# A four-layer metaformer on one core: the first and last chunk of each mixer rewritten, and the feed-forward stages put in another order

## The chip, the core and the metric

The kernel runs on one core of one Trainium2 chip. Its time is the device time in microseconds (us) of one execution; three runs of the kernel before gave 8925.73, 8928.08 and 8933.33 us, median 8928.08. The core has a TensorE (PE) with a separate record for its weight loads (PEld), a VectorE (DVE), a ScalarE (ACT), a GpSimd (POOL) and a SyncE (SP) that mostly issues DMAs. Each engine works its own instructions in the order of its queue and waits on semaphores for the others. "L578" is line 578 of the kernel before.

## What is computed

An input of 64 images, each of 11 x 11 = 121 positions with 128 values, goes through four layers, all in fp32:

```python
for l in range(4):
    x = x + mixer[l](layernorm(x))
    x = x + ffn[l](layernorm(x))
```

The mixer is the same in all four layers. It treats the 121 positions as channels and 256 inner features as the time axis of a recurrence with 16 states, for two sets k of parameters:

```python
xc, z = split(x @ in_proj_w.T)                 # 256 features each
t = silu(conv1d(xc, conv_w) + conv_b)          # three taps over the 121 positions, 256 -> 256
dt, B, C = split(einsum(t, x_proj_w[k]))
delta = softplus(dt @ dt_proj_w[k] + dt_proj_b[k])
h = scan(exp(delta * A[k]), delta * B * t)     # along the 256 features; 121 channels x 16 states
y[k] = (h * C).sum(states) + Ds[k] * t
yn = layernorm(y[0] + flip(y[1]))              # over the 121 channels
out = (yn * gelu(z)) @ out_proj_w.T
```

The feed-forward part differs. Layer 0 has 64 experts that choose their tokens: a gate of 128 x 64, a softmax over the 121 tokens of an image, the top 8 tokens of each expert pooled, an MLP 128-512-128 for each expert, and its output spread back over those tokens. Layers 1 and 2 have an RNN: `wx = BatchNorm(x @ W.T)`, then `y[t] = sigmoid(wx[t] + y[t-1] @ V.T)` over the 121 positions. Layer 3 is a spectral transform: the positions fall into four bands (0-15, 15-30, 30-60, 60-121), each with convolutions by 16 filters and their sign-alternated twins, channel matrices M for each filter, three autoregressive terms M_u, and weights for the bands that are made from a softmax.

## The kernel before

The mixer (class `Conv`) works through the 64 images in eight chunks of 8 images. For each chunk and each k, the 121 channels are taken two at a time (8 images x 16 states = 128 partitions for a channel), 61 pairs, which gives 2 x 8 x 61 = 976 steps to a layer. A step makes `delta` for its pair in PSUM with two bf16 products (`rows`, L557), `exp(delta * A)` with two ACT instructions (`exps`, L570), multiplies the drive by B on POOL (`times_b`, L546, one instruction for two steps), and runs one scan of 512 elements on DVE (`scan`, L578) into a buffer `H`. PE then multiplies by C and sums the states (`by_c`, L599), `keep_y` (L614 on DVE, L616 on ACT) gathers this in `yst`, and `store_y` (L631) writes it to a DRAM tensor `yD`. The drive comes back from DRAM copied 16 times (`load_u`, L534, tile `ub`); `load_r` (L507) and `load_bc` (L516) fetch delta, B and C.

What feeds a chunk is made in three groups of closures. `lead(c)` loads the images (`begin`, L190), takes mean and variance on DVE (L196, L201), makes the reciprocal root by `rsqrt` (Ln at L175, Exp at L176), normalises on ACT, transposes on PE, copies on ACT, and then runs the convolution: for each image four products into a PSUM tile `pc` (three taps and one with the bias row, L232), for each two images a copy to `t` (`convd`, L235), and silu for all (`silu`, L239). `steps(c, k, start, apart, late)` makes delta for four pairs of images: `project` (PE, L267), `parts` (relu and abs, L274), `e` (exp, L277, and +1, L279), `ln` (L283), `less` and `delta` (DVE, L286 to L290), `first` (bf16 part of delta, L295), `u` (POOL, L299), `rest`, `second`, `third` (the two further bf16 parts, L302 to L308), `store` (two DMAs, L311 and L312, to `dD` and `uD`). Each closure has a step number, and `apart` says how many steps lie between one pair of images and the next. The PSUM tile `pd` has one buffer and is held from `project` to `delta`. `aside(c)` makes B and C (product L333, copy L338, store L341 to `bcD`) and the Ds term (L351 to L361, stored to `sD`). What follows a chunk is `gate` (gelu(z)) and `tail(c)`: load of the Ds term (`ts`, L411) and of y (L413), transposes to a PSUM tile `pk`, sum and layer norm of y (L426 to L448), product with the gate (L453), load of x (`xo`, L462), output projection (L472), addition (L475) and store to a DRAM tensor `mid` (L485), in four blocks, one for each half of the features and each half of the images.

Inside the mixer the program order is the order written by hand (`manual_schedule`). In the loop, the closures of the next chunk and of the chunk before are laid between the 976 steps by `lay` and `lay_at`. Only two places are not beside the loop: the first chunk of a layer, ahead of step 0,

```python
self.do([begin] + norms + convs)
self.do([f for _, f in self.steps(0, 0, 0, 8, 1)] + aside[: 3 * CB // 2])
```

and the last chunk's `tail`, behind step 976. `apart` is 8 in this call, `late` is 1. A layer begins with the mixer's constants (`weights`, L95 to L148: twelve loads and the products made of them) and its buffers (L155 to L166, with memsets of `da`, `yst` and others).

The feed-forward functions run without a written order; a scheduler orders their instructions by priority, which falls in program order. X, all 64 images, is loaded in eight DMAs at L1159 (each of 8 images, directly behind the mixer), and stored in eight at L1162. `layer_norm` (L46 to L58) normalises 8 images in eight instructions, the last at L58. `moe_layer` runs the gate for groups of 8 images (L784 to L814) on 64 partitions, then the experts (L820 to L846), then the output (L851 to L858). `rnn_layer` runs a front over groups of 8 images (product with W at L886 to L890, batch statistics, `wx` copied by ACT), puts `wx` into PSUM with products of 512 columns (L914), and then runs the 121 steps: product with V (L920) and sigmoid (L923). `stu_layer` loads filters, M_u and a weight matrix W, and for each group of 8 images: layer norm and transposes, the products with the filters (`pu`, L1072) and with M (`acc`, L1075, L1077), and four products of W (L1092) with 2048 columns of M, written to a DRAM tensor `KD` (L1094); then three bands whose matrices are read back from `KD` (L1106), and the addition into X for all images (L1127 to L1129).

## Time and profile before

The profiled execution took 8938.7 us; its span is 8936.9 us, at a mean granted TensorE clock of 0.754. The table gives where its parts lie in us from the start of the span. The channel loop is counted from its first scan (L578) to its last.

| layer | ahead of the first scan | channel loop | last chunk, to the last store of mid | feed-forward part, to its last store |
|---|---|---|---|---|
| 0 | 0 - 108.4 | 108.4 - 1767.7 | - 1817.1 | - 2223.0 (experts) |
| 1 | 2223.0 - 2330.5 | - 3984.2 | - 4036.7 | - 4285.0 (RNN) |
| 2 | 4285.0 - 4392.8 | - 6052.0 | - 6101.5 | - 6348.7 (RNN) |
| 3 | 6348.7 - 6465.2 | - 8113.0 | - 8163.0 | - 8936.9 (spectral) |

Over the whole span the busy shares are:

```profile
PE 6165.8 (69%) x83464; PEld 3518.2 (39%) x83464; DVE 6233.4 (70%) x8294; ACT 5776.4 (65%) x12747; POOL 5849.9 (65%) x3155
```

A window's line in what follows gives its start and end, its length, then the busy time of each engine in it with the number of instructions in brackets, the granted PE clock as a share of the full one, the mean busy share of the 16 DMA engines, and GB/s. A timeline's line gives the start of an instruction, its duration, its engine and line, the operation, output and inputs, and in square brackets how long the engine had been idle before it and what ended that.

### The profile page before, as it was taken

The page shows a single profiled execution, that of the slowest core. Times are in us where ns is not written, and L with a number is a line of the kernel's source. Part 1 is how long each engine was busy: PE and PEld are TensorE (multiplying, and loading weights), DVE is VectorE, ACT ScalarE, POOL GpSimd, SP SyncE. Part 2 cuts the span into 40 slices and gives each one's busy share as a digit, 9 for nine tenths or more (in the row PEclk, how much of TensorE's full clock was granted, in tenths as well). Part 3 has the DMA queues.
Part 4 walks back from the last instruction along what each step waited for, and adds up shares of the span by engine and source line. Part 5 has one row for each costly group of instructions (what it writes and reads, how often), then busy time and mean ns, then how long its engine had stood idle before and what let it go on. Part 6 is the DMA issues. An engine that isn't in the chain of part 4 may idle for free. (4 is left out here: it accounts for less than half of the span.)

```text
span 8936.9 us, 208810 instructions
## 1 busy us (share of the span) xinstructions
PE 6165.8 (69%) x83464; PEld 3518.2 (39%) x83464; DVE 6233.4 (70%) x8294; ACT 5776.4 (65%) x12747; POOL 5849.9 (65%) x3155
## 2 busy tenths in 40 slices
PE   5667767637567777766577777765567777765998
PEld 2333434327233434333234444443334444433445
DVE  5888888753588888872478888883288888884220
ACT  5888888631688878862478887872288788873210
POOL 5888888700588888860488888880188888892000
PEclk7777777657677777775687777775577777777999
DMA  6889898815688899970489999991288999994111
GB/s 148 213 227 223 225 222 227 195 55 166 152 220 225 225 222 224 228 183 25 128 215 219 224 225 222 223 227 41 61 218 225 228 226 224 224 234 106 35 32 42
DMA packets 926426, 1604.62 MB, mean 180 GB/s; under 512 B 139455, under 2 KB 611587, under 8 KB 923587
## 3 DMA queue, kind: packets, MB, share of 16 engines
q1 hardware_dynamic: 924171, 1589.17, 71.1%
q8 instruction: 655, 10.73, 0.5%
q14 instruction: 320, 2.62, 0.1%
q10 hardware_dynamic: 1280, 2.10, 0.1%
HBM read 1300.49 MB, written 290.52 MB: 178 GB/s over the span
## 5 line engine op out<-in xcount | busy, mean ns | idle before, releaser
L546 POOL TENSOR_TENSOR ub<-ub,Bt 128x1024 f32<-128x1024 f32 (+1 forms) x1984 | 4563.0, 2317 | 770.6 <-DMA ub<-uD 544.5
L578 DVE TENSOR_TENSOR_SCAN H<-da,ub 128x512 f32<-128x512 f32 (+1 forms) x3904 | 4499.2, 1200 | 229.4 <-POOL ub L546 104.3
L570 ACT ACTIVATE da<-da,A 128x255 f32<-128x255 f32 x7744 | 3390.5, 446 | 1112.9 <-PE da L557 938.2
L557 PE MATMUL da<-R,pick 120*128 120x255 bf16 x7744 | 1793.5, 326 | 885.6 <-DVE H L578 708.3
L599 PE MATMUL yb<-H,Cz 128*16 128x64 f32 x65536 | 1734.5, 251 | 548.8 <-ACT yst L616 361.0
L599 PEld LDWEIGHTS yb<-H,Cz 128*16 128x16 f32 x65536 | 1173.6, 111 | 1597.1 <-issue 844.5
L557 PEld LDWEIGHTS <-pick 120*128 120x128 bf16 x7744 | 601.0, 104 | 1590.4 <-issue 818.1
L161 POOL MEMSET t<- 128x2048 f32 x4 | 7.2, 1805 | 914.4 <-DMA mid<-X 914.4
L232 PE MATMUL pc<-w_conv,xnT 128*121 128x256 f32 x1536 | 502.7, 431 | 65.7 <-ACT t L235 65.7
L614 DVE TENSOR_TENSOR yst<-yst,yb 128x512 f32<-128x512 f32 (+2 forms) x640 | 342.0, 552 | 274.5 <-PE yb L599 274.0
L299 POOL TENSOR_TENSOR u<-relu,t 128x512 f32<-128x512 f32 x256 | 327.3, 1279 | 294.8 <-DVE relu L290 294.8
L267 PE MATMUL pd<-t,w_dt 122*128 122x512 f32 x512 | 392.9, 861 | 130.1 <-ACT t L239 68.5
L616 ACT COPY yst<-yb 128x512 f32<-128x512 f32 (+2 forms) x640 | 330.5, 542 | 107.6 <-DMA yD<-yst 47.6
L286 DVE SCALAR_TENSOR_TENSOR pd<-w,pd 128x512 f32<-128x512 f32 x256 | 175.8, 687 | 301.7 <-ACT w L279 301.7
L308 POOL TENSOR_TENSOR d<-relu,d 128x512 bf16<-128x512 f32 x256 | 297.0, 1160 | 80.5 <-ACT d L305 80.2
L232 PEld LDWEIGHTS pc<-w_conv,xnT 128*121 128x121 f32 x1536 | 273.7, 210 | 130.8 <-ACT t L235 96.5
L453 POOL TENSOR_TENSOR y<-y,g 128x484 f32<-128x484 f32 x128 | 155.5, 1215 | 240.4 <-ACT y L448 240.4
L302 POOL TENSOR_TENSOR relu<-relu,d 128x512 f32<-128x512 f32 x256 | 297.3, 1161 | 7.8
L333 PE MATMUL pb<-t,x_bc 121*64 121x512 f32 x256 | 184.5, 811 | 133.7 <-ACT bc L338 102.7
L1055 DVE COPY U<-pu 128x488 f32<-128x488 f32 x128 | 85.3, 667 | 273.6 <-PE pu L1072 273.6
L523 POOL TENSOR_TENSOR Cz<-Cp,own 128x512 f32<-128x512 f32 x256 | 274.4, 1072 | 0.0
L1057 ACT COPY U<-pu 128x488 f32<-128x488 f32 x128 | 72.8, 569 | 296.5 <-PE pu L1072 296.5
(211 smaller groups left out, 7529.1 us busy)
## 6 DMA issues: line engine op xcount, KB each, us to landing
ub<-uD SPq DMA_DIRECT2D x1920, 512.0 KB
dD<-d SPq DMA_DIRECT2D x256, 384.0 KB
R<-dD SPq DMA_DIRECT2D x192, 420.0 KB
uD<-u SPq DMA_DIRECT2D x256, 256.0 KB
sD<-s SPq DMA_DIRECT2D x128, 256.0 KB
ts<-sD SPq DMA_DIRECT2D x64, 512.0 KB
yD<-yst SPq DMA_DIRECT2D x512, 60.5 KB
y<-yD SPq DMA_DIRECT2D x128, 242.0 KB
```

The costliest lines, as they stand in the source:

```text
L232: nc.tensor.matmul(pc, lhs, rhs, start=(j == 0), stop=(j == 3))
L267: nc.tensor.matmul(s["p"], self.w_dt[:, k, :], tb[: D + 1], start=True, stop=True)
L299: nc.gpsimd.tensor_mul(s["u"], s["relu"], tb)
L302: nc.gpsimd.tensor_sub(s["relu"], s["relu"], s["d"][:, 0, :])
L308: nc.gpsimd.tensor_sub(s["d"][:, 2, :], s["relu"], s["d"][:, 1, :])
L546: self.nc.gpsimd.tensor_mul(x, x, self.bc[m, "Bt"].unsqueeze(1).to_broadcast([128, n, L]))
L557: self.nc.tensor.matmul(self.da[g % RING][:, j, 1:], self.pick[:n, d % 5].rearrange("p n b -> p (n b)"), self.R[m, d // 35][:n, d % 35 // ...
L570: self.nc.scalar.activation(x, x, AF.Exp, scale=self.A[:, m % 2, d : d + 1])
L578: self.nc.vector.tensor_tensor_scan(self.H[dq % 2][:, :n, p - DQ[dq][0]], self.da[g % RING].rearrange("p j l -> p (j l)")[:, :n], x.rearra ...
L599: self.nc.tensor.matmul(self.yb[32 * q : 32 * q + 16, slot % 8, :, :, :w], self.Cz[slot // 8][:, place % 64 : place % 64 + 2, :].rearrange ...
L614: nc.vector.tensor_add(dst, dst, src)
L616: nc.scalar.copy(dst, src)
```

## The change

**Layer norm of the feed-forward parts.** `layer_norm` takes mean and variance with `bn_stats` and `bn_aggr`, one of each for an image, makes the reciprocal root with Ln and Exp, and normalises with one ACT instruction for an image.

**Constants.** `weights` is cut into the loads (`weights`) and what is made of them (`made`). The feed-forward functions get an argument `load`: called in them, it issues the loads of the next layer's mixer constants, and then the eight loads of X. `made()` runs inside the feed-forward part. `cw`, `cs` and `cv` are their pools.

**First chunk of a layer.** The two `H` buffers serve as scratch memory (`spare`), as the scan doesn't use them yet. The convolution has three taps and four PSUM buffers (`da`), the bias is added by DVE from a tile that a broadcast DMA fills, and silu is done for two images at a time. In `steps` the four pairs of images each have their own PSUM and SBUF tiles and stand 2 steps apart, with the closures of B and C among them. `da`'s first column is cleared after that, and `yst` no longer.

**Last chunk of a layer.** `last` takes the place of `tail(NC - 1)`: loads of `ts` and `xo` one step after the loop's end, `load(0)` (y of the first half of the features) at step 12 after it, transposes and the gate's half of the projection (`ahead`) before `load(1)`, and four blocks skewed against each other (`finish`).

**Experts.** The gate works on 128 partitions (four images for each half) and goes through the groups with norm, front, softmax and back each one group apart; two multiplications of a group go to POOL, one copy from ACT to DVE. The pool of expert weights has four buffers for three. The output part is loaded in quarters and goes by row halves.

**RNN.** The front is skewed by one group, and `wx` is copied by DVE. In layer 2, the new function `stu_matrices` makes the matrices of layer 3's spectral part: 64 products of W with 256 columns of M, one of them issued after each step of the recurrence, written to `cx.KD`.

**Spectral part.** The products with W and their loads are gone from it, `scale_weights` is taken out into a function, the layer norm and transposes of a group run one group ahead, the last group's products come after the bands, X of the other groups is added before them, and the K tiles have three buffers for two.

```diff
 def layer_norm(cx, pool, dst, src, eps):
-    nc.vector.reduce_sum(mean, src, axis=AX.X)
...
-    nc.vector.tensor_mul(dst, dst, bcast(rstd, C))
+    for i in range(G):
+        nc.vector.bn_stats(st[:, i, :], src[:, i, :])
+    for i in range(G):
+        nc.vector.bn_aggr(mv[:, i, :], st[:, i, :])
+    nc.scalar.activation(r[:, 0, :], mv[:, :, 1], AF.Ln, bias=eps[:D])
+    nc.scalar.activation(r[:, 0, :], r[:, 0, :], AF.Exp, scale=-0.5)
+    nc.vector.scalar_tensor_tensor(r[:, 1, :], mv[:, :, 0], -1.0, r[:, 0, :], ALU.mult, ALU.mult)
+    for i in range(G):
+        nc.scalar.activation(
+            dst[:, i, :], src[:, i, :], AF.Identity, bias=r[:, 1, i : i + 1], scale=r[:, 0, i : i + 1]
+        )
...
 # Conv.lead
+        taps = 3 if c == 0 else 4
...
+            if c == 0:
+                s["bias"] = self.spare[0][:D, :L]
+                nc.sync.dma_start(s["bias"], self.cx.a[f"L{self.l}_conv_conv_b"].to_broadcast([D, L]))
...
-                s["pc"] = self.ps_d.tile([D, 2, L], F32, name="pc", tag="pd")
+                s["pc"] = self.da[b // 2][:D] if c == 0 else self.ps_d.tile([D, 2, L], F32, name="pc", tag="pd")
...
         def convd(b):
-            nc.scalar.copy(self.t[:D, b : b + 2, :], s["pc"])
+            if c > 0:
+                nc.scalar.copy(self.t[:D, b : b + 2, :], s["pc"])
+                return
+            bias = s["bias"].unsqueeze(1).to_broadcast([D, 2, L])
+            nc.vector.tensor_add(self.t[:D, b : b + 2, :], s["pc"], bias)
...
 # Conv.steps
+        alone = c == 0 and k == 0
...
+                if alone:
+                    at = 1024 * b + 512 * ("relu", "abs", "w", "ln").index(n)
+                    return self.spare[1][:, at : at + 512]
...
+                if alone:
+                    s["p"] = self.da[b // 2].rearrange("p j l -> p (j l)")
+                else:
+                    s["p"] = self.ps_d.tile([128, 512], F32, name="pd", tag="pd")
...
 # Conv.last, new
+        def sides():
+            for q in range(2):
+                nc.sync.dma_start(ts[q], self.sD[c, :, 4 * q : 4 * q + 4, :])
...
+        def load(h):
+            for q in range(2):
+                nc.sync.dma_start(s[q, h]["y"], self.yD[c, 128 * h : 128 * h + 128, q * D4 : q * D4 + D4])
...
+        def finish():
...
+            for k in range(6):
+                if k < 4:
+                    b = s[blocks[k]]
+                    nc.vector.tensor_add(b["y"], b["y"], b["pk"][:, :D4])
...
+                    self.rsqrt(b["r"], b["mv"], self.cx.eps5)
+                if 0 < k < 5:
+                    q, h = blocks[k - 1]
...
+                    nc.gpsimd.tensor_mul(b["y"], b["y"], self.g[:, h, q * D4 : q * D4 + D4])
+            for q in range(2):
+                proj(q, True)
+                nc.sync.dma_start(self.dst(c * CB + 4 * q, 4), xo[q].rearrange("p (b c) -> p b c", c=C))
...
 # Conv.run
-        self.do([f for _, f in self.steps(0, 0, 0, 8, 1)] + aside[: 3 * CB // 2])
+        bc = [(3 * i // 3 + 1.5, f) for i, f in enumerate(aside[: 3 * CB // 2])]
+        self.do([f for _, f in sorted(self.steps(0, 0, 0, 2, 1) + bc, key=lambda x: x[0])])
+        for x in self.da:
+            self.nc.vector.memset(x[:, :, 0:1], 0.0)
...
+        sides, load, ahead, finish = self.last(NC - 1)
+        self.at(G + 1, sides)
+        self.at(G + 12, lambda: load(0))
...
-        self.do([f for _, f in sorted(self.tail(NC - 1), key=lambda x: x[0])])
+        ahead()
+        load(1)
+        finish()
...
 # moe_layer
+        xn, pr = {0: norm(0)}, {}
+        for g in range(NG + 2):
+            if g + 1 < NG:
+                xn[g + 1] = norm(g + 1)
+            if g < NG:
+                pr[g] = front(xn[g])
+            if 1 < g:
+                back(g - 2, xn[g - 2])
+            if 0 < g <= NG:
+                softmax(g - 1, pr[g - 1])
+            if g == 1:
+                made()
...
 # stu_matrices, new: 8 rounds of 2048 columns, called by next(beside, None) after each step of layer 2's recurrence
+            for j in range(0, CC, PC):
+                pa = ps.tile([R0[3], PC], F32, name="pa", tag="mm")
+                nc.tensor.matmul(pa, W, loaded[c0][:, j : j + PC], start=True, stop=True)
+                nc.vector.tensor_copy(ka[:, j : j + PC], pa)
+                yield
+            nc.sync.dma_start(cx.KD[:, c0 : c0 + CC], ka)
...
 # stu_layer
+        end = NB - GB
+        u = turned_in(0)
+        for b0 in range(0, end, GB):
+            ahead = turned_in(b0 + GB)
+            last_band(b0, u)
+            u = ahead
...
+        for b0 in range(0, end, GB):
+            turned_out(b0)
+        last_band(end, u)
+        turned_out(end)
...
 # metaformer_kernel
+            def load():
+                made = weights() if l < 3 else None
+                for b0 in range(0, NB, GB):
+                    nc.sync.dma_start(cx.X[:, b0 : b0 + GB, :], mid[2 * l][:, b0 : b0 + GB, :])
+                return made
+            FFN[l](cx, l, load)
```

## The prediction

> **What bounds the kernel now.** I read the page first (no engine above 70% of the span, the chain of waits spread thin), then asked for busy time by stretches. The stretches show two kinds of stage. In each of the four layers the channel loop of 976 steps looks like this:
>
> ```profile
> core 0: us, PE busy (x) PEld busy (x) DVE busy (x) ACT busy (x) POOL busy (x), PEclk, DMA share, GB/s
> 108.40:1767.70 1659.30, 1156.00 (x19612) 651.49 (x19611) 1406.42 (x1775) 1315.54 (x2930) 1438.67 (x767) 0.76 0.89 221
> 2330.50:3984.20 1653.70, 1151.10 (x19612) 648.20 (x19611) 1406.49 (x1775) 1315.97 (x2930) 1438.93 (x767) 0.77 0.89 221
> 4392.80:6052.00 1659.20, 1162.17 (x19612) 654.66 (x19611) 1406.26 (x1774) 1315.36 (x2930) 1439.11 (x768) 0.76 0.91 221
> 6465.20:8113.00 1647.80, 1150.02 (x19612) 650.74 (x19611) 1406.07 (x1775) 1315.74 (x2930) 1438.94 (x768) 0.77 0.89 222
> ```
>
> DMA share 0.9, DVE and POOL 85%: four engines and the queues are full together. These sum to 6620 us of 8937. The other 2317 us are the stages between the loops, where nothing is full:
>
> ```profile
> 1767.70:1817.10 49.40, 16.89 (x80) 14.47 (x80) 12.31 (x44) 8.38 (x24) 4.82 (x4) 0.62 0.28 72
> 1817.10:2047.00 229.90, 88.79 (x288) 56.68 (x288) 116.60 (x288) 66.65 (x85) 0.00 (x0) 0.51 0.16 47
> 2047.00:2177.00 130.00, 125.95 (x1025) 121.84 (x1024) 32.93 (x48) 22.44 (x34) 0.00 (x0) 0.93 0.73 227
> ...
> 2223.00:2330.50 107.50, 48.73 (x116) 22.32 (x117) 20.55 (x49) 40.42 (x72) 18.56 (x17) 0.60 0.22 60
> ...
> 4036.70:4125.00 88.30, 45.59 (x96) 21.17 (x97) 52.14 (x71) 35.23 (x51) 0.00 (x0) 0.50 0.19 60
> ...
> 6189.50:6327.70 138.20, 105.02 (x273) 69.54 (x273) 6.56 (x15) 26.98 (x121) 0.00 (x0) 0.50 0.00 0
> ...
> 8222.30:8683.80 461.50, 460.80 (x1150) 211.36 (x1150) 127.08 (x181) 92.90 (x161) 0.00 (x0) 1.00 0.12 29
> ```
>
> In order: last chunk of layer 0; the gate of its experts; the experts' products (PE-bound); first chunk of layer 1; the front of a recurrent layer; its recurrence; the groups of the spectral layer (PE-bound). In the first, second, fourth and fifth the busiest engine is at 34 to 59%: engines take turns. Two places of the timeline show why:
>
> ```profile
> 2237.83 0.30 SPq L190 DMA_DIRECT2D x<-mid  x1
> ...
> 2279.48 0.60 ACT L274 ACTIVATE relu<-pd 128x512 f32<-128x512 f32 x1
> ...
> 2284.22 2.08 PE L267 MATMUL pd<-t,w_dt 122*128 122x512 f32 x2 [4.88 <-DVE relu L290]
> ...
> 4257.13 0.69 PE L920 MATMUL pst<-ys,VT 128*128 128x64 f32 x2 [0.31 <-ACT ys L923]
> 4257.86 0.22 ACT L923 ACTIVATE ys<-pst 128x64 f32<-128x64 f32 x1 [0.78 <-PE pst L920]
> ```
>
> The next projection of the first chunk waits until the previous pair of images has left DVE; a recurrence step (1.00 us) leaves PE 0.31 us idle.
>
> **What the Trainium skill says.** "TensorE: Matmul & The Clock Gate", Part 1, has the PE clock gated at half or full rate, released by some 3.4 us of dense work. The trace agrees: the recurrence is granted 0.50, the dense spectral groups 1.00, and in layer 3's first chunk six L232 instructions take 2.92 us cold and 1.56 us later. "ScalarE: Activation LUTs", Table sets, says that ln and exp share a set; the tables here cost 1283 ns a load (What ACT_TABLE_LOAD costs says the same), and the trace of layers 1 to 3 loads twice, at L175 and L176.
>
> **The change, part by part.** A plus is time saved, against the profiled execution (8938.7 us, span 8936.9).
>
> *First chunk, four times.* In layer 1 mid is stored by 2223.0, x is issued at 2237.83, the convolutions run from 2254.0, the first relu is at 2279.48, the loads behind the last bcD store start at 2320.58, the first scan at 2330.49.
> With the weights made in the FFN, x can go at about 2223.4: +14.4. The set is loaded ahead, so two table loads go: +2.6. Convolutions: three taps are 2 x 1.56 us a pair of images and, with four PSUM buffers, four pairs run without the wait for the copy, 12.5 us; then a DVE add 0.7, silu 0.6, table 1.3: 15.1 for 25.5, +10.4.
> Steps two apart: ACT holds 4 x 4.0 us (relu, abs, exp, add, ln, two casts from the rows) plus 4 x 0.57 us of bc copies, 18 us; POOL 4 x 3.57 us, starting after the first delta at about 9.5 us. So the last store is about 25 us after the first projection, 23 after the first relu; 2 us for it to land: 25 for 41.1, +16. Each wait in this order stands on in-order queues, so I allow 8 us either way. Sum +43 for layers 1 and 2. Layer 0 has its setup on the path still: 10.4 + 16 + about 6 for x past the setup's buffers, +32. Layer 3 ran its convolutions cold (30 us for 20): +45. Sum **+163**.
>
> *Last chunk, four times.* Now 1767.7 to 1817.1: stores of yD issued to 1775, then ts, then four blocks that each wait for the one before. After: ts and xo are issued before the stores. Half 0 of yD is stored by 1769.4, load(0) waits about 2.5 us for it, and holds SP: the other eight stores (0.7 us each) are queued behind it and end at 1778.4, load(1) is in by about 1784.5. Two blocks are done by then. The other two: DVE 2 x 2.25 us, scale 0.6, normal 1.63 twice on ACT, POOL 1.2, to 1793.7; projections 3.6 us cold each behind, add 0.75: last store at 1800. **+17 each, +68.** From both sides: 10 if load(0) lands late, 22 if PE is warm.
>
> *Constants ahead of X.* X(0) was issued 0.36 us after the last store. Now SP issues first the FFN's constants and the next layer's twelve: 18 in layer 0, 15 in layer 1, 37 in layer 2 (22 are the spectral filters'). At the start of the kernel twelve took 7.3 us (0.74 to 8.07, with a gap where the queue was full). So 12, 10 and 22 us: **-44**. All of LN waits for X(0), and everything else for LN; nothing covers this. Bounds: -25 (issue time of 0.35 us alone) to -60 (the 4-byte rows of sg, whose landings are 8 us on the chain of waits).
>
> *Gate of the experts.* 225.3 us from X (1822.8) to pooled (2048.1), groups strictly in turn. After, for a group: DVE 8 stats 1.65, 8 aggr 1.75, shift 0.17, three reductions and differences of half the elements 1.95, reciprocal 0.16, max and replace 1.8 (3.6 for eight now), copy 0.69: 8.2 us. ACT 0.48 + 3.2 + 1.14 + 0.66 + 0.6 + 1.04 = 7.1. PE transposes 2.1, gate 3.8, back 0.9, pooling 3.7 cold with two waits of 0.6 and one of 0.75: 12.4, about 7 warm. I take 11.5. LN 8.4, first 6, seven at 11.5, drain 17, the weights of layer 1 made there 5: 117. **+108** (85 to 125). The expert products stay: PE busy 126 of 130 us, a fourth buffer gives nothing. Output stage: two gaps of DMA and DVE, **+5**.
>
> *Recurrent layers.* Groups already take 7.65 us (L58 to L58) of which DVE has nearly all; after, 3.57 + 2 x 0.67 + 2 copies of wx at 0.7 to 1.0, 6.5 to 6.9. With made() 3 us: **+8 each, +16.** Layer 2's recurrence gets 64 products of 256 columns. From L914 (512 columns, 2.02 us, which lengthens its step by 1.13) a cold one is 1.0 us against 0.31 idle: +0.4 a step, 26 us lost. But PE is then busy without a gap, and by the clock page should warm; L1092 warm gives 0.5 us, which fits. I take **-8** (0 to -26). The m loads are 8 MB in 120 us, no load on the queue.
>
> *Spectral layer.* Products with W leave the groups: L1092 is 30.1 us busy in a stage where PE never rests, +27 with the group that lay outside. The stall at 8211 to 8222 behind the W chain goes, +10. The KD write and read ahead of the bands (8683.8 to 8693.7), +10; two shorter K waits, 2.7 and 2.8 us, +4. Last X: 8911.2 to 8936.9 is 25.7 us of adds and stores for all groups, now for one (about 8.5), +17. X behind 3.8 MB of phi, M and MU, -4. **+64.**
>
> Sum: 163 + 68 - 44 + 108 + 5 + 16 - 8 + 64 = **+372**. The loops are left alone. 8938.7 - 372 = 8567; the median of the runs shown lies 10.6 us below the profiled execution, so 8556.
>
> **The rivals.** *Covered less (8635):* in-order queues keep the skewed groups at PE's cold chain (85 for 108), the steps of the first chunk lose 8 us a layer (32), the recurrence stays cold (18 more): 73 plus a few us. For it: granted 0.50 and 0.51 in these stages. Against: fewer gaps mean a warmer clock.
> *Warm everywhere (8480):* gate groups at 8.5 us (+21), convolutions at full clock in every layer, last chunk 22 us, X delayed by issue time alone (+19), recurrence steps shorter than 1.00 us: about +75. For it: the second half of layer 3's convolutions did warm.
> *Slower than before (above 8946):* the loop gets longer. It has 3904 steps of 1.70 us; 0.1 us more a step (6%) eats the 372 us, and above that decides. Its place would be the ub broadcast (ub waits for its DMA 544 us now) if tiles at new addresses or the early reuse of H delayed it. Against: no instruction inside the steps changes, and what is added comes after step 976.
> *Not doing what it says:* the scheduler outside the channel loop may already have overlapped the groups, so that program order moves nothing. The gate's timeline speaks against it: DVE idle 14 us in a group. It would leave some 250 us (8680).
>
> **How the numbers follow.** Main case 0.58, less covered 0.20, warm 0.14, no overlap 0.04, slower 0.03, and 0.01 for no change. Less than 0.2% (18 us) can't be told from no change. The main case's own bounds (8 a layer, 15 for constants, 20 for the gate, 10 for the rest) reach 45 us to either side; with the two neighbours the range is 8460 to 8645. Faster 0.96, same 0.01, slower 0.03.
>
> **What would show it.** First scans 65 us after mid is stored; 33 us from the last yst to the last mid store; X's first LN later than now against that store; gate stage near 117 us; L920 steps of layer 2 at about 1.0 us with the clock above 0.8; no L1092 in the last stage. Loop stretches other than 1650 to 1660 us would make the prediction wrong at its root, and a gate stage above 160 us its largest term.

## The result, and the profile after

The changed kernel takes 8556.44 us (median of four runs, 8551.45 to 8578.09), against 8930.61 us before (8925.73 to 8933.33). The ratio is 0.9586 with a 95% interval of 0.9569 to 0.9604. The forecast was 8556. That the two agree this closely is luck: six of its eight terms are off by 16 to 29 us, in both directions, and the errors happen to cancel.

The profiled execution took 8578.1 us, span 8576.3, so it shows 360.6 us less than the one before. The table sets it out by stage, with the same marks in both traces (first scan, last write of `yst`, last store of `mid`, issue of X(0), last store of the feed-forward part). The ends of the channel loops in the table of the kernel before are the last writes of `yst` too, not the last scans; its feed-forward ends lie 5 to 7 us behind the ones used here, where the last store had landed.

| stage | forecast | before | after | saved |
|---|---|---|---|---|
| first chunks, layers 0 to 3 | +163 | 108.4, 112.8, 115.1, 122.9 | 81.7, 77.8, 78.6, 80.9 | +140 |
| channel loops | 0 | 6617.8 | 6625.7 | -8 |
| last chunks | +68 | 50.4, 53.5, 49.6, 50.9 | 28.7, 31.4, 30.2, 30.4 | +84 |
| last store of mid to X(0) | -48 | 0.0, 0.0, 0.1, 0.4 | 9.9, 9.5, 34.9, 17.1 | -71 |
| experts (gate: 230.7 to 110.4) | +113 | 400.3 | 271.7 | +129 |
| RNN, layer 1 | +8 | 240.8 | 204.0 | +37 |
| RNN, layer 2 | 0 | 240.8 | 258.1 | -17 |
| spectral part | +68 | 773.3 | 705.7 | +68 |

(The forecast's 64 for the spectral part held 4 us of delay for X; here they stand with the constants; the last row runs to the end of the span.) Nothing inside the steps of the loop differs between the kernels, but the loop of one and the same layer differs by 14 to 16 us over the fourteen traces of this study. So the -8 of all four loops says nothing, and in what follows the parts are compared by stage and not by whole times alone.

The stretches of the changed kernel that answer to those shown before, in the same columns: last chunk of layer 0, gate, products of the experts, first chunk of layer 1, front of layer 1's RNN, recurrence of layer 2 and what stands behind it, groups of the spectral part.

```profile
core 0: us, PE busy (x) PEld busy (x) DVE busy (x) ACT busy (x) POOL busy (x), PEclk, DMA share, GB/s
1738.90:1767.60 28.70, 12.50 (x80) 11.81 (x80) 13.09 (x53) 7.95 (x24) 4.83 (x4) 0.67 0.25 66
1777.50:1888.00 110.50, 71.68 (x271) 40.98 (x270) 55.06 (x273) 55.19 (x127) 17.90 (x16) 0.67 0.43 114
1888.00:2019.00 131.00, 126.82 (x1024) 122.63 (x1024) 32.97 (x48) 21.39 (x33) 0.00 (x0) 0.92 0.67 209
2049.30:2127.00 77.70, 27.81 (x84) 15.44 (x85) 14.75 (x40) 34.38 (x63) 18.38 (x17) 0.64 0.32 87
3824.90:3874.80 49.90, 38.82 (x110) 18.46 (x108) 40.80 (x170) 38.73 (x104) 0.00 (x0) 0.84 0.32 83
5903.00:6043.00 140.00, 107.16 (x304) 72.08 (x304) 13.64 (x32) 26.88 (x120) 0.00 (x0) 0.57 0.17 41
6043.00:6088.00 45.00, 37.38 (x146) 30.34 (x145) 27.19 (x56) 0.22 (x1) 0.00 (x0) 0.86 0.66 197
7892.00:8282.00 390.00, 386.79 (x969) 179.14 (x969) 88.96 (x187) 102.95 (x193) 0.00 (x0) 0.99 0.02 6
```

Read the fifth line against the one before the change (88.3 us, PE 45.6, clock 0.50). PE has no less to do and was busy for 38.8 us, but it is granted 0.84 where it was granted 0.50, and the stretch is 38 us shorter. (Both lines end a few us ahead of the first sigmoid.) Read the sixth and seventh for what went wrong: the recurrence has a clock of 0.57 and is no shorter than before, and behind it lie 45 us where layer 1 has 16.

### The profile page after: what moved, and what is told of

Read it like the earlier page. It is cut to its first block, busy times and chain, and to the rows that moved or that the text cites. A ratio compares the mean times of both kernels' runs of the same rounds, so it can differ in the third digit from the quotient of the medians.

```text
span 8576.3 us, 209337 instructions
## 1 busy us (share of the span) xinstructions
PE 6028.0 (70%) x83432; PEld 3462.5 (40%) x83432; DVE 6122.9 (71%) x8654; ACT 5803.0 (68%) x12946; POOL 5868.7 (68%) x3171
## 4 chain that ended last, share of the span: by engine, by line
PE 31%; ACT 20%; DMA 18%; DVE 14%; issue 8%; POOL 7%; SPq 2%; DVEq 0%; POOLq 0%; ACTq 0%
DVE H L684 8%; ACT da L676 7%; DMA ub<-uD 5%; POOL ub L652 5%; PE yb L705 4%; PE da L663 4%; DMA ts<-sD 4%; PE pc L244 3%; DMA uD<-u 3%; PE acc L1290 3%; PE out L1329 2%; PE pu L1287 2%; PE pst L1186 2%; PE po L500 2%; DMA R<-dD 2%
## 5 line engine op out<-in xcount | busy, mean ns | idle before, releaser
L244 PE MATMUL pc<-w_conv,xnT 128*121 128x256 f32 x1344 | 445.5, 429 | 56.4 <-ACT t L248 56.4
L295 PE MATMUL pd<-t,w_dt 122*128 122x512 f32 x480 | 355.4, 832 | 57.4 <-ACT t L255 57.4
L327 POOL TENSOR_TENSOR u<-relu,t 128x512 f32<-128x512 f32 x240 | 307.4, 1281 | 22.2 <-DVE relu L318 22.2
L336 POOL TENSOR_TENSOR d<-relu,d 128x512 bf16<-128x512 f32 x240 | 279.0, 1163 | 59.2 <-ACT d L333 59.2
L330 POOL TENSOR_TENSOR relu<-relu,d 128x512 f32<-128x512 f32 x240 | 279.3, 1164 | 6.6
L244 PEld LDWEIGHTS pc<-w_conv,xnT 128*121 128x121 f32 x1344 | 234.7, 209 | 103.4 <-ACT t L248 82.2
L401 PE MATMUL pg<-xnT,in_zT 128*128 128x484 f32 x256 | 156.2, 695 | 110.1 <-ACT g L412 101.2
```

Source lines behind the costliest of these rows:

```text
L244: nc.tensor.matmul(pc, lhs, rhs, start=(j == 0), stop=(j == taps - 1))
L295: nc.tensor.matmul(s["p"], self.w_dt[:, k, :], tb[: D + 1], start=True, stop=True)
L327: nc.gpsimd.tensor_mul(s["u"], s["relu"], tb)
L330: nc.gpsimd.tensor_sub(s["relu"], s["relu"], s["d"][:, 0, :])
L336: nc.gpsimd.tensor_sub(s["d"][:, 2, :], s["relu"], s["d"][:, 1, :])
```

## Experiments

Each kernel was run against the kernel before on the same chip; times are medians. Four chips were used, on which the kernel before took 8929.5 to 8939.7 us, so a difference between whole times from two of them is sure to some 10 us only. Two expectations quote a front "to the first sigmoid" of 49.9 (after) and 86.5 us (before); these were read at the table load ahead of that sigmoid. Read at the sigmoid itself, as below and in the later expectations, they are 53.4 and 90.1, with the same difference.

### 1. X ahead of all constants

```diff
+            for b0 in range(0, NB, GB):
+                nc.sync.dma_start(cx.X[:, b0 : b0 + GB, :], mid[2 * l][:, b0 : b0 + GB, :])
             def load():
                 made = weights() if l < 3 else None
-                for b0 in range(0, NB, GB):
-                    nc.sync.dma_start(cx.X[:, b0 : b0 + GB, :], mid[2 * l][:, b0 : b0 + GB, :])
                 return made
```

> The changed kernel with the eight loads of X issued ahead of all constants again, nothing else moved. In the changed kernel X(0) is issued 9.9, 9.5, 34.8 and 16.8 us behind the last store of mid in layers 0 to 3, 71 us in sum. Theory (these 71 us lie on the path, as the prediction's term of -44 says, only larger): X(0) is issued within 1 us of the last store, and 55 to 70 us go, to about 8490 us. Rival (the constants are needed as early as X, so the delay only moves to the first product with WT or the gate, and to made()): less than 25 us go, 8530 us or more.

8503.8 us, 53 less. X(0) now goes out up to 1 us ahead of the last store. From that store to the end of the feed-forward part, layers 0 to 3 gain 12.5, 3.1, 34.4 and 10.9 us, 61 in all, inside the theory's bounds, while the whole time misses them by 2 us. So the delay was on the path, but not all 71 us of it: in layer 1 only 3 of 9.5 us come back, as PE then waits 8.1 us for WT, which has moved behind X.

### 2. Four buffers for d and u in the first chunk

```diff
-                s["d"] = work.tile([128, 3, 512], BF16, name="d", bufs=2)
+                if alone:
+                    at = 3072 + 768 * (b // 2)
+                    d = self.spare[0][:, at : at + 768].bitcast(BF16)
+                    s["d"] = d.rearrange("p (s l) -> p s l", s=3)
+                else:
+                    s["d"] = work.tile([128, 3, 512], BF16, name="d", bufs=2)
...
+                if alone:
+                    s["u"] = self.spare[0][:, 1024 + 256 * b : 1536 + 256 * b]
```

> The changed kernel with four buffers for the tiles d and u in the first chunk's first set of steps (they lie in the other H buffer; two buffers before). Theory (the steps of the first chunk fell behind the forecast because pairs 2 and 3 wait for the stores of pairs 0 and 1: ACT 4.2 and 4.5 us, POOL 2.7 and 2.7 us in layer 2): the time from the first projection to the issue of the last uD store falls from 34.5 us to 26 or 28, 7 us in each layer, about 28 us in all, to 8528 us. Rival (ACT's order and the stores on SP hold the chain anyway): under 2 us in each layer, no change that can be told.

8534.4 us; first chunks 78.0, 72.7, 75.6 and 76.2 us, 3.0 to 5.1 us shorter, 16.5 in all. This is more than the rival's 2 us and some half of the theory's 7. From the first projection to the issue of the last store of u it is 29.0 us for 34.4, where the theory said 26 to 28. In the changed kernel, layer 1's end, ACT's timeline has

```profile
4077.48 0.61 ACT L333 CAST d<-H 128x512 bf16<-128x512 f32 x1
4082.31 0.62 ACT L323 CAST d<-H 128x512 bf16<-128x512 f32 x1 [4.22 <-DMA dD<-d]
...
4088.46 0.62 ACT L323 CAST d<-H 128x512 bf16<-128x512 f32 x1 [4.53 <-DMA dD<-d]
```

and with four buffers (the same casts are L328 and L341 there)

```profile
4050.20 0.61 ACT L341 CAST H<-H 128x512 bf16<-128x512 f32 x1
4050.70 0.62 ACT L328 CAST H<-H 128x512 bf16<-128x512 f32 x1
4053.18 0.62 ACT L341 CAST H<-H 128x512 bf16<-128x512 f32 x1 [1.85 <-POOL H L338]
```

The waits for the store of d are gone, and POOL's subtractions end what is left of them.

### 3. The products really between the steps

```diff
-        for t0 in range(0, D, TS):
+        with tc.manual_schedule():
+            for t0 in range(0, D, TS):
```

> The changed kernel with the recurrence of the RNN in its written order, so that each of the 64 products for the distance matrices follows one step. In the changed kernel the scheduler put them in bunches, 8 ahead of the recurrence, 16 in two bunches inside it and 40 behind it; from the issue of X(0) to the last store of the part layer 2 takes 258.2 us, layer 1, which has no such products, 204.0. Theory (the products were not hidden because they were not between the steps): layer 2 falls to 205 to 220 us, 40 to 50 us less, 8510 us. Rival (a product between two steps lengthens the step by its whole duration, about 0.6 us for 64 steps, as PE is the bound of a step): layer 2 stays at 245 us or more, under 13 us less.

8529.6 us; layer 2's feed-forward part falls from 258.1 to 216.4 us, 41.7 less, as the theory has it, though the whole time, 27 us less, misses the 8510 that it named. What the scheduler made of the written order stands in PE's timeline of the changed kernel (each product is two instructions):

```profile
5897.07 1.68 PE L1098 MATMUL pa<-m,W 128*105 128x256 f32 x6
5899.43 2.67 PE L1098 MATMUL pa<-m,W 128*105 128x256 f32 x10 [0.68 <-DVE wx L1138]
...
5940.43 4.67 PE L1098 MATMUL pa<-m,W 128*105 128x256 f32 x16
...
5992.45 3.69 PE L1098 MATMUL pa<-m,W 128*105 128x256 f32 x8
...
5999.63 1.89 PE L1098 MATMUL pa<-m,W 128*105 128x256 f32 x8
...
6043.13 11.42 PE L1098 MATMUL pa<-m,W 128*105 128x256 f32 x40
6055.81 1.98 PE L1098 MATMUL pa<-m,W 128*105 128x256 f32 x8 [1.26 <-DVE ka L1099]
6061.15 5.36 PE L1098 MATMUL pa<-m,W 128*105 128x256 f32 x16 [3.36 <-DMA KD<-ka]
6068.68 5.36 PE L1098 MATMUL pa<-m,W 128*105 128x256 f32 x16 [2.17 <-DMA KD<-ka]
```

Eight products stand ahead of the recurrence, two bunches of eight (the second in two halves) stop it for some 5 us each, and 40 follow when it is over. None is hidden in a step. In the written order PE's timeline, while it has products to put in and behind the last of them, and the stretches of the first and second half of the recurrence are:

```profile
5930.36 0.43 PE L1187 MATMUL pst<-ys,VT 128*128 128x64 f32 x2
5930.64 0.63 PE L1098 MATMUL pa<-m,W 128*105 128x256 f32 x2
5931.11 0.43 PE L1187 MATMUL pst<-ys,VT 128*128 128x64 f32 x2
...
5975.95 0.43 PE L1187 MATMUL pst<-ys,VT 128*128 128x64 f32 x2 [0.31 <-ACT ys L1190]
5976.69 0.43 PE L1187 MATMUL pst<-ys,VT 128*128 128x64 f32 x2 [0.31 <-ACT ys L1190]
...
5978.96 0.69 PE L1187 MATMUL pst<-ys,VT 128*128 128x64 f32 x2 [0.31 <-ACT ys L1190]
5979.96 0.69 PE L1187 MATMUL pst<-ys,VT 128*128 128x64 f32 x2 [0.31 <-ACT ys L1190]
```

```profile
5909.00:5972.00 63.00, 55.59 (x264) 35.50 (x264) 29.24 (x69) 13.89 (x62) 0.00 (x0) 0.96 0.70 180
5973.00:6036.00 63.00, 47.34 (x131) 31.56 (x132) 3.86 (x10) 12.54 (x56) 0.00 (x0) 0.54 0.04 14
```

With a product in every gap PE is granted 0.96, and most steps take 0.75 us, product included; without them, in the second half, most take 1.00 us at 0.54. It is the clock that does this: behind the last product, steps with an empty gap still take 0.75 us until the full clock is withdrawn at 5978.47, and 1.00 us from then on, with the same 0.31 us of waiting for ACT in both. Not all of it is gain. Every eighth step, where the next columns of `wx` are put in, takes 2.79 us for 2.13, as their scaling on DVE stands behind the copy of the last product and PE waits 1.06 us for it. The recurrence with 64 products takes 128.4 us from first to last sigmoid, layer 1's without any 134.6 in the changed kernel and 135.9 in this run: the added work makes it shorter.

### 4. The new layer norm alone

The kernel before with nothing exchanged but `layer_norm`, as the diff of the change has it.

> The kernel before with nothing changed but layer_norm of the feed-forward parts (bn_stats, bn_aggr, Ln and Exp, eight ACT instructions). The RNN front of layer 1 (issue of X(0) to the first sigmoid) took 86.5 us before and 49.9 in the changed kernel, 36.6 less where 8 were forecast. Theory 1 (the layer norm was what was mis-sized: 2.3 us of DVE for a group where 3.6 were reckoned): most of it comes from layer_norm alone, the front falls to 65 us or less. Theory 2 (the skew of one group did it, as PE and ACT no longer take turns): the front stays above 72 us, the gate of the experts, 230 us before, at 195 us or more, and the total is 8850 to 8900 us.

8909.0 us, ratio to before 0.9978 (0.9970 to 0.9986). The RNN fronts fall by 1.9 and 2.5 us to 88.2 and 87.6, the gate by 11.4 to 219.3, the spectral part not at all. Theory 2, though the total lies 9 us above its bound. DVE's work in the front of layer 1 fell from 54 to 32 us, and the front stayed where it was: DVE was not its bound. The gate lost something else as well. In the kernel before, ACT loaded a table ahead of the norm's Sqrt (L56) and another ahead of the softmax's Exp (L793) in seven of its eight groups, 14 loads of 1.28 us; with Ln and Exp in the norm none of them is left. The fronts had one such load at L56. This may be why the gate gains 11 us and the fronts 2; the two were not run apart.

### 5. The gate and the RNN's front in plain order

```diff
-        xn, pr = {0: norm(0)}, {}
-        for g in range(NG + 2):
...
+        for g in range(NG):
+            xn = norm(g)
+            pr = front(xn)
+            softmax(g, pr)
+            back(g, xn)
```

and in the RNN likewise `norm`, then for each half transposes, copy, product and `leave`.

> The changed kernel with the gate of the experts and the fronts of the RNNs in plain order again: norm, front, softmax and back of a group behind one another, each half of a group through the RNN's front on its own. The layer norm, the 128 partitions of the gate, POOL's share and wx on DVE stay. The gate (issue of X(0) to the last write of pooled) takes 110.5 us in the changed kernel, 230 in the one before; the front of layer 1 (issue of X(0) to the first sigmoid) 49.9 and 86.5. Theory (the skew is what took the time out, as the layer norm alone gave 3 us in an RNN and 11 in the experts): the gate goes back to 150 us or more, the front to 70 us or more, 70 to 110 us lost in all. Rival (the scheduler finds the overlap by itself once layer norm and the wx copy are split as they are now): gate under 125 us, front under 56.

8652.2 us, 96 more. The gate takes 178.7 us, layer 1's front 72.5 (68.9 where the expectation reads it, a little under the theory's bound). Of the gate's 120 us, 68 are the skew's and 52 come from layer norm, 128 partitions and POOL; of the front's 37, 19 are the skew's and 18 the rest's. This holds for undoing the skew last; layer norm alone gave 11 and 2 us (experiment 4), and the other parts were not run apart. The two stretches, layer 1's front first:

```profile
3880.10:3952.60 72.50, 53.81 (x113) 26.09 (x112) 45.98 (x180) 41.97 (x106) 0.00 (x0) 0.50 0.19 57
1774.00:1952.70 178.70, 90.66 (x270) 53.68 (x268) 56.17 (x273) 55.81 (x127) 17.56 (x16) 0.50 0.25 70
```

The clock is back at 0.50 in both, and the same work of PE takes 53.8 us for 38.8 and 90.7 for 71.7. The skew gives twice: engines overlap, and PE is granted more. In plain order PE's stretches without a gap of 0.1 us are at most 2.9 us long in the front, most of them with 0.65 to 0.71 us between, and the clock never leaves 0.50. With the skew most are 4.0 to 5.3 us long with 0.3 us or less between, and from 3843.35 the full clock is granted for 30.7 us on end.

### 6. The old ends of the mixer

```diff
-        self.do([f for _, f in sorted(self.steps(0, 0, 0, 2, 1) + bc, key=lambda x: x[0])])
+        self.do([f for _, f in self.steps(0, 0, 0, 8, 1)] + aside[: 3 * CB // 2])
...
-        ahead()
-        load(1)
-        finish()
+        self.do([f for _, f in sorted(self.tail(NC - 1), key=lambda x: x[0])])
```

> The changed kernel with the two ends of the mixer undone in part: the last chunk goes through tail again, and the first chunk's steps stand 8 apart with B and C behind them, the convolution stays new. In the changed kernel the stretch from the last yst to the last store of mid takes 28.7 to 31.4 us (49.6 to 53.5 before), and from the last store of the layer before to the first scan 77.8 to 80.9 us in layers 1 to 3. Theory (prediction: 17 us for the last chunk, 16 for the steps): last chunk 47 to 53 us, first chunk 92 to 98, 35 to 38 us lost a layer, 145 in all. Rival (stores and loads on SP bound both ends, so the order of the arithmetic is worth little): last chunk under 40, first chunk under 86.

8617.6 us, 61 more, not 145: the theory fails in size at both ends. The last chunk itself is back at 52.6 to 63.1 us, but now the scheduler puts the constants and X(0) between its stores (X(0) goes out 19 to 37 us ahead of the last of them in layers 0 to 2). From the last write of `yst` to the end of the feed-forward part the layers lose 9.3, 12.1, -4.4 and 11.5 us. So of the 84 us that the last chunk got shorter, 28 are left when the constants may hide under the old one. The first chunks lose only 5.0 to 8.1 us, and that is not the distance of the steps: from the first projection to the last store of u (layer 2) 8 apart takes 33.5 us, 2 apart 35.1. The kernel before took 31.7 us from the first relu to the issue of the last store of u, the changed one 31.6 and this one 30.0, so neither the distance nor the four PSUM tiles moved it by more than 2 us. What moved are B and C: with them behind the steps their last store is 71.9 us from the layer's start, with them among the steps 55.5. The distance and the place of B and C were not run apart.

### 7. The mixer's constants back where they were

```diff
-                made = weights() if l < 3 else None
...
+        if l < 3:
+            v, kept, passing, weights = mixer(l + 1)
+            weights()()
```

> The changed kernel with the mixer's constants loaded and made at the start of each mixer again, as before the change (behind the load of x, where the scheduler puts them). Theory (prediction: loading them ahead saves 14 us of the first chunk and costs 10 to 20 us ahead of X): X(0) is issued within 2 us of the last store in layers 0 and 1 and some 22 us behind it in layer 2, and the first chunks of layers 1 to 3 are 12 to 16 us longer, so that the whole is the same within 15 us. Rival (beside the load of x, 8.7 us to the first layer norm, the constants cost next to nothing): the first chunks are less than 6 us longer and the whole is 20 to 30 us shorter than the changed kernel's, 8530 us.

8572.6 us, the changed kernel's time within what can be told. The first chunks of layers 1 to 3 are 12.8, 13.8 and 12.2 us longer, and from the last store of mid to the end of the feed-forward part layers 0 to 2 are 13.0, 10.9 and 12.1 us shorter. X(0) goes out 2.5, 0.4 and 16.8 us behind the last store, where 2, 2 and 22 were expected. The theory holds: the constants were moved from one place on the path to another.

### 8 to 12. Together, and what else stood in the way

Experiment 8 joins 1 (behind the few constants that the first products need), 2 and 3, and takes ACT's `second` one place earlier.

> The changed kernel with four parts together: X ahead of all constants but the few that the feed-forward part's own first products need; four buffers for d and u in the first chunk, and ACT's second bf16 part of delta one place earlier; the 64 products between the recurrence's steps. Theory (the three terms are in different stages and add up: 60 for X, 17 for the buffers and some 10 for ACT's order, 42 for the recurrence): about 130 us less than the changed kernel, 8430 us, X(0) within 3 us of the last store, layer 2's feed-forward part at 215 us, first chunks near 71 us. Rival (constants that come behind X delay made() and the products with WT, and the load of M collides with them): 90 us or less, 8465 us or more.

8449.3 us, 107 less than the changed kernel, between theory and rival. The terms add up where nothing else lies behind: first chunks 72.0 to 72.7 us, layer 2 at 221.5. But layer 1 gains nothing by the early X (213.0 us from last store to the end of the part, 213.5 before), as `made`, which stands ahead of the recurrence, now waits (PE 5.4 us for a constant at L140), and layer 2's front grows to 81.6 us.

Why layer 2's front was 74.4 us in the changed kernel and layer 1's 53.4 is seen in ACT's timeline there:

```profile
5859.27 1.28 ACT L56 ACT_TABLE_LOAD   x1
5860.56 0.30 ACT L56 ACTIVATE ln_r<-ln_mv,eps 121x8 f32<-121x8 f32 x1
5860.77 0.54 ACT L1154 COPY xT<-pt 128x484 f32<-128x484 f32 x1
5861.33 1.28 ACT L57 ACT_TABLE_LOAD   x1
```

```diff
-    nc.scalar.activation(sq, sq, AF.Sqrt)
-    nc.scalar.activation(sq, sq, AF.Sqrt)
+    nc.scalar.activation(sq, sq, AF.Ln)
+    nc.scalar.activation(sq, sq, AF.Exp, scale=0.25)
```

> The changed kernel with the fourth root of sigma (matrices of the spectral part, made in layers 2 and 3) taken as Exp(0.25 Ln) where it was two Sqrt. In the changed kernel the front of layer 2 (issue of X(0) to the first sigmoid) takes 74.3 us, that of layer 1 53.4, and ACT loads a table ahead of each Ln and each Exp of layer 2's layer norms, 16 loads of 1.28 us, and 14 in layer 3. Theory (the Sqrt pushes out the set that holds both Ln and Exp, and the loads set ACT's pace: 2 x 1.28 us for each of eight groups, 20.5 us): no such loads are left, layer 2's front is at 53 to 57 us, layer 3 gains 3 to 6 us ahead of its first products, the whole 8533 us. Rival (layer 2's front waits for the 22 loads of filters and for the loads of M): the front stays above 67 us.

8535.9 us. Layer 2's front is at 55.4 us, no such load is left, and the spectral part takes 696.1 us for 705.7: the theory, with 10 us in layer 3 where 3 to 6 were expected. The same piece of the timeline:

```profile
5848.90 0.29 ACT L56 ACTIVATE ln_r<-ln_mv,eps 121x8 f32<-121x8 f32 x1
5849.09 0.54 ACT L1154 COPY xT<-pt 128x484 f32<-128x484 f32 x1
5849.54 0.21 ACT L57 ACTIVATE ln_r<-ln_r 121x8 f32<-121x8 f32 x1
```

> The combined kernel (X ahead of the constants, four buffers for d and u, products between the steps) with the two changes to ACT's tables: the fourth root by Exp and Ln, and a load of the set of Ln and Exp pinned behind the arrival of x in the first chunk, so that L183 and L184 load none. The combined kernel took 8449 us. Theory: 7.7 us in layer 2's front, where it had six such loads, 2.6 us in each of three first chunks, a few us in layer 3, about 18 us in all, 8431 us. Rival (ACT waits for x or for constants at these places, so the loads lie in its idle time): under 6 us.

8441.4 us (8416.1 to 8459.7), too wide a spread for a verdict on 18 us; by stage the part of layer 2 loses 10.4 us, the first chunks 0.7 to 2.7, layer 3 nothing. But layer 1's part, which had no such load to lose, loses 6.0 us as well, so stages of these kernels differ by some us without an edit of theirs.

> The same, with the 22 small loads and the making of W moved out of layer 2 into layer 1's feed-forward part, where they stand behind X and its constants; W is kept over the mixer of layer 2. In the combined kernel layer 2's front took 81.6 us, as ACT and PE stood waiting in it 4.7, 5.8 and 8.6 us for constants that come behind these loads. Theory: layer 2's front falls to 58 to 63 us, like layer 1's (61.6), and layer 1's grows by less than 4, 8412 us in all. Rival (layer 1's front takes over the same waits, as its last steps are queued behind W's): the sum of the two fronts stays within 8 us of what it was.

8422.2 us, ratio 0.9431 (0.9417 to 0.9445), the fastest median, but its interval overlaps that of the run before. The rival holds: layer 2's front falls by 13.9 us to 57.1 and layer 1's grows by 11.6 to 67.3.

Experiment 12 has the loads of the constants issued by `nc.gpsimd` where it was `nc.sync`.

> The combined kernel with the two table changes (8441 us), and the constants of layers 1 to 3's mixers, of W and of the spectral part issued by POOL instead of SP, so that X and these constants no longer stand in one queue; POOL is idle in these stretches. So far, whichever stood first made the other late: X first took 71 us of delay from X and gave back 8 to 15 us in each of the fronts of layers 1 and 2 and in front of the first spectral products (36.9 us from X(0) for 17.7). Theory (SP's queue, in issue time and in its waits when it is full, is what they share): the front of layer 1 is at 52 to 55 us (55.7), that of layer 2 at 55 to 60 (71.0), the first spectral product 18 to 24 us behind X(0), 8405 us or less. Rival (the 16 DMA engines are what they share, or a DMA issued by POOL costs more than one by SP): layer 2's front stays above 66 us and the first spectral product behind 30, no gain or a loss.

8480.0 us, 39 more than experiment 10 (35 by the ratios to the kernel before, as the chips differ). The rival: fronts at 59.2 and 92.3 us, first spectral product 42.4 us behind X(0). Who POOL's issues waited for, in layer 2 (line, what for: us in total, times, longest):

```profile
POOL F L1070 <- DMA sg<-in_sgn_dram: 10.4, 2, 5.7
POOL out_wT L99 <- DMA conv_wT<-in_L_conv_conv_wT_dram: 4.8, 1, 4.8
...
POOL x_dt L99 <- DMA sg<-in_sgn_dram: 3.4, 1, 3.4
```

and SP's in the changed kernel, ahead of X(0) of the same layer:

```profile
SPq L1059 <- DMA sg<-in_sgn_dram: 5.5, 2, 3.2
SPq L99 <- DMA sg<-in_sgn_dram: 4.7, 2, 3.3
```

Whichever engine issues them, the next loads wait for earlier ones to land, above all for the `sg` rows, 960 single floats of 4 bytes each. 10.2 of the 34.9 us ahead of X(0) are these waits. The Trainium skill ("DMA: Bandwidth & Descriptors", Issuing engines are not separate DMA queues) says that issuing from several engines saves the issue time alone; this run agrees in that the second issuer brought no gain. Which of the rival's two grounds holds, the shared engines or the cost of POOL's issues, is not told apart. `sg` as one wide load was not tried.

## Why the forecast came out, term by term

The total was right to within what can be measured, and most of the mechanisms were, but the total owes its closeness to luck: -23, +16, -23, +16, +29 and -17 us cancel, and so do the 11 us by which the profiled execution missed its forecast (8578.1 for 8567) and the distance of that execution from the median (21.7 us, where 10.6 were taken). By the steps of the forecast:

- **RNN fronts, +16, failed in layer 1 (+37).** The step was "groups already take 7.65 us (L58 to L58) of which DVE has nearly all". The starts of L58 lie between 1.4 and 17.8 us apart, 8.7 in the mean, and 7.65 is one of them; DVE was busy for 52.14 of the 88.30 us in the forecast's own line, and waited otherwise. The group rows of the front, before and after, say so in their last column:

```profile
L894 DVE BATCH_NORM_STATS2 stats<-pw 128x6 f32<-128x484 f32 x16 | 10.7, 670 | 26.3 <-PE pw L893 26.3
```

```profile
L1137 DVE BATCH_NORM_STATS2 stats<-pw 128x6 f32<-128x484 f32 x16 | 10.4, 651 | 2.0 <-PE pw L1157 2.0
```

  26.3 us of idle time behind PE's product became 2.0. And the new layer norm was charged with 3.57 us a group; it takes some 2.3 (L52 1.56, L54 0.54 and L58 0.15, from 3830.42 on), as the price of `bn_aggr` came from the first chunk, where its eight take 1.75 us with their result in PSUM. Groups are now 4.6 us apart. By its own figures, too, the working gives 6 to 9 us for the eight groups, so 3 to 6 with `made`, and not 8.
- **Layer 2's recurrence, -8 (0 to -26), failed as -17 net of a front that should have gained.** The step took for granted that each product goes between two steps. For products that do, it was right that PE warms and a little too cautious on the step: it is 0.75 us for the most part and not 1.00, and the recurrence gains 6 us over layer 1's. But the order was left to the scheduler, outside `manual_schedule`, and the program didn't do what it says (experiment 3). The rival of that kind was held against the gate, where it is wrong, and not here. The second loss, the tables (19 us), was not foreseen at all.
- **Constants ahead of X, -48, were -71.** Layers 0 and 1 came as said (9.9 and 9.5 us for 12 and 10). Layer 2 took 34.9 us for 22: the 22 small loads 16.5, as the landing of `sg` was given only as the far bound, and the twelve behind them 17.9, where twelve take 7.4 us in layer 0. These three sum to 54 us and lie within the bound of -60. The rest is layer 3, with 17.1 us for 4; there the issues of M and MU alone take 4.9 and 7.7 us of SP, and no wait for a landing is shown ahead of them:

```profile
7857.90 4.93 SPq L1248 DMA_DIRECT2D M<-n_L_ffn_M_phi_minus_dram  x1
7862.88 7.66 SPq L1252 DMA_DIRECT2D MU<-in_L_ffn_M_u_dram  x4
7870.58 6.21 SPq L1392 DMA_DIRECT2D X<-mid  x8
```

  That "nothing covers this" was right for 61 of the 71 us (experiment 1), and what the step bought, 13 us a first chunk, is what it cost (experiment 7).
- **First chunks, +163, were +140.** The early x and the convolutions came as worked out (first convolution to first relu of layer 2 14.3 us, forecast 15.1). The steps gained 9 of 16 us (first relu to last store 32.2 us, forecast 23), and those 9 by the place of B and C alone: the last store of u is no nearer to the first relu than before. The forecast had counted the four PSUM tiles as four pairs in flight, where d and u still had two buffers; four of them give back 16.5 of the 23 us (experiment 2). And the two table loads per layer (+2.6) stayed in layers 1 to 3. The Trainium skill ("ScalarE: Activation LUTs", Table sets) gives one load for ln and then exp; these traces show that only where the common set is already loaded, and a load before each of the two otherwise.
- **Last chunks, +68, were +84** by their own stretch, 28.7 to 31.4 us for 33; but experiment 6 shows that 28 of it is what the whole gains over the old order, once the constants are there to fill it.
- **Gate, +108, was +120**, at 11.6 us a group for 11.5 taken; the start and the drain were shorter. The 14 table loads that left this stage (experiment 4) are not named in the forecast. The output stage came as forecast.
- **Spectral part, +68, was +68,** but by luck: it lost some 10 us to table loads that nobody foresaw (experiment 9), so the other terms brought some 10 more than forecast. Which of them did stays open.
- Of the signs that the forecast named, the first scan was late (78 to 81 us from the issue of the last store; the 65 of the forecast count from its landing and are some 70 by this mark), the steps of layer 2 have 1.00 us but a clock of 0.57 and not above 0.8, and the others came as said: the loops at 1654 to 1657.5 us, no product with W in the last stage, X's first layer norm later.

## What to carry to other kernels

An order written in a program is a wish where a scheduler places the instructions: look up in the trace where the filler went before it is counted as hidden. When stages take turns, skewing them can pay twice if PE is among them: here it was granted 0.84 and 0.67 for 0.50. A gap filled with other products can cost less than an empty one. Loads that are moved ahead of or behind one another may only change who waits: the mixer's constants cost X what they gave the first chunks, while X ahead of them gave back 61 of 71 us, and little of that in layer 1. So ask for each load who needs it first, remove what makes the queue wait, and look for the table loads that a single foreign function brings into a loop.

## What was not expected of the hardware

A recurrence step of 1.00 us (0.69 us of PE, then a sigmoid of 0.22) became 0.75 us with 0.63 us of PE work put into it, at a granted clock of 0.96 for 0.54. Two Sqrt ahead of a loop of Ln and Exp led to 16 loads of 1.28 us inside it. And loads of single floats held up the issue of unrelated loads by up to 3.3 us each on SP and 5.7 on POOL.
